# Layer 0 of a four-layer network: column-bias queries stored column by column, and the preparation of a unit in pieces of one copy

## The chip, the cores and the metric

The kernel runs on one core of a Trainium2 chip. The core has five engines with a queue each: TensorE (PE in the profile; PEld are its weight loads), VectorE (DVE), ScalarE (ACT), GpSimd (POOL) and SyncE (SP, which here only issues transfers). Each engine works through its own queue in order; semaphores order the engines among each other. Matrix products land in PSUM, which has eight banks; everything else lies in SBUF. The metric is the time of one execution in microseconds on the device, the median of several runs. Everything is computed in float32.

## The reference, cut to what matters

Four layers work on `x` of shape (2, 64, 64, 128). The change touches layer 0 alone: group norm, then attention over the 4096 positions of each image with 4 heads of 32 values, with a relative position bias of rows and one of columns:

```python
x = x + _L0_conv_ref(_gn(x), L0_conv_w_qkv, L0_conv_pos_emb_h, L0_conv_pos_emb_w)

def _L0_conv_ref(x, w_qkv, pos_emb_h, pos_emb_w):
    scale = 1.0 / float(kd) ** 0.5
    qkv = jnp.einsum('bhwc,cd->bhwd', x, w_qkv)
    q, k, v = jnp.split(qkv, [qk_dims, 2 * qk_dims], axis=-1)
    ...
    pos = relative_position_bias(pos_q, pos_emb_h, pos_emb_w).reshape(B, nh, L, L)
    scores = jnp.einsum('bnqd,bnkd->bnqk', q, k) * scale + pos
    attn = jax.nn.softmax(scores, axis=-1)
    out = jnp.einsum('bnqk,bnkd->bnqd', attn, v)
```

The bias of a query at row x, column y, for a key at row x', column y', is the query times the row embedding of x'-x plus the query times the column embedding of y'-y. So the row bias of a query is one number for each of 64 key rows, and the column bias one for each of 64 key columns.

## The kernel before

**Units and steps.** Layer 0 is `layer0` (a prologue), then `l0_bounded` (the loop). The loop has 8 units: image `b`, pair of heads, half of the queries (2048, that is 32 rows of 64). A unit has 4 blocks of 512 queries, a block 32 steps of 128 keys: 1024 steps. A step is: scores on TensorE (L615: 64-by-64 tiles, both heads, into two PSUM banks), their exponential on ACT (L623), a product with the exponentiated column bias on DVE (L626), and, two steps later, the product with the values on TensorE (L573). After 32 steps ACT copies the sums out (L582), and three small pieces finish the block (`l0_finish`).

The row bias needs no pass of its own: rows 32 to 63 and 96 to 127 of the query operand `qa` hold it, and the same rows of the key operand `ka` hold a one at the key's row (`l0_hot`, on POOL). The column bias comes in as a factor: its exponential `ew`, for 64 key columns, is multiplied in by L626.

**The preparation of a unit**, `l0_prepare`, is a generator: it stops at every `yield`, and each `piece()` of the loop runs it to the next one. It makes the operands of the next unit while the present one runs:

- queries: L657 projects two blocks of 512 positions into one bank (`l0pq`); L677 to L687 copy it into `qa`: to rows 0-31 and 64-95 as the operand proper, for both halves of the keys, and to rows 32-63 (query columns 0 to 31) and 96-127 (columns 32 to 63) as the operand of the column bias, in the same order of positions;
- column bias: for each of the 64 query columns L701 multiplies a slice of the embedding with the queries of that column (`rhs=qa[lo : lo + HD, :, y::S]`, one value in 64). Columns 0-31 come from rows 32-63 and go to one bank, columns 32-63 come from rows 96-127 and go to another; both use partitions 0-63 of their bank. L712 exponentiates each bank into `ew`, with the positions interleaved. Once all are done, a transfer on SP's queue (L715) doubles `ew` to the other 64 partitions;
- row bias: L723 multiplies for each of 32 rows, from rows 0-31 into partitions 0-63 and from rows 64-95 into partitions 64-127 of one bank (`l0ph`); L734 copies it into rows 32-63 and 96-127 of `qa`, over the copies that the column bias was made from;
- for the first half of a pair also the keys: L657 (`l0pk`) and L747, L748.

The loop calls `piece()` after every odd step; after steps 2, 6, 10 and so on it calls `more()`, which runs other generators that wait in `extra` (L1's first rows, `statistics` of finished blocks). Finishing pieces go ahead of preparing ones. PSUM in the loop: 4 banks for scores, 2 for the sums, 2 shared by everything else (`misc`).

The order on a queue isn't the order written: a planner with its own model of the engines orders each block of the program, and moves an instruction ahead where it finds the engine free. It also orders two engines that read one PSUM bank, one after the other.

**The prologue.** `Net.__init__` loads `x` with 8 transfers of 512 KB on SP's queue (L52). `layer0` loads the weights and the two embeddings on ACT's queue (L264, L282), turns the embeddings (L286) and copies them to four groups of partitions (L289), and works out an upper bound of all scores (L300 to L354; a Gram matrix of the weights and the lengths of the embeddings). For each image it then transposes `x` in 8 banks (`group_block`: L113, statistics on DVE L116, a copy on ACT L118), aggregates the statistics (`group_stats`) and normalises two halves (L395). `lengths` squares a half (L373 on POOL or L375 on ACT) and finds its longest row. In between, `pieces(4)` runs the generator of the first unit. The bound decides at run time whether `l0_bounded` or `l0_any` runs; here it is the former. Last come the values of image 0, `l0_values` (L484, L491). PSUM in the prologue: 5 banks, all under `misc`.

Of the kernel before, what the change touches and what calls it, by code (L numbers as in the profile page):

```python
# [14 lines left out]
P = 128  # L15
B = 2
# [23 lines left out]
class Net:  # L40


    def __init__(self, ctx, tc, ins, out):
# [6 lines left out]
        src = ins["x"].rearrange("b h w c -> (b h w) c").rearrange("(g p) c -> p g c", p=P)  # L50
        for g in range(0, B * NC, 8):
            nc.sync.dma_start(out=self.x[:, g : g + 8, :], in_=src[:, g : g + 8, :])  # L52
# [16 lines left out]


# [186 lines left out]
    def layer0(self, xT, gst, na, nb):  # L257
# [3 lines left out]
        with ExitStack() as st:  # L261
            wp = st.enter_context(tc.tile_pool(reuse_waits="tile", name="l0w", bufs=1))
            w = wp.tile([P, 3 * C], F32, tag="wqkv", name="wqkv")
            nc.scalar.dma_start(out=w, in_=ins["L0_conv_w_qkv"])  # L264

# [9 lines left out]
            with (  # L275
                tc.tile_pool(reuse_waits="tile", name="l0s", bufs=2) as ap,
                tc.tile_pool(reuse_waits="tile", name="l0sp", bufs=5, space=PSUM) as ps,
            ):
                raw = ap.tile([P, 2, HD], F32, tag="raw", name="l0raw")
                nc.vector.memset(raw, 0.0)  # L280
                for i, n in enumerate("hw"):
                    nc.scalar.dma_start(  # L282
                        out=raw[: 2 * S - 1, i, :], in_=ins[f"L0_conv_pos_emb_{n}"]
                    )
                    pt = ps.tile([P, 512], F32, tag="misc", name=f"l0pe{n}")
                    nc.tensor.transpose(pt[:HD, :P], raw[:, i, :], self.ident)  # L286
# [3 lines left out]
                posq = ap.tile([P, 2, HD], F32, tag="posq", name="l0posq")  # L290
                nc.vector.tensor_tensor(posq, raw, raw, ALU.mult)
                posn = ap.tile([P, 2], F32, tag="posn", name="l0posn")
                nc.vector.tensor_reduce(posn, posq, AX.X, ALU.add)
# [40 lines left out]
                for j in range(2):  # L334
# [25 lines left out]
                made = {}  # L360
                first = self.l0_prepare(
                    ps, (0, 0, 0), xT, w, pe, [ka], (qe[:, 0], qe[:, 1]), made
                )

                def pieces(n):
                    for _ in range(n):
                        next(first, None)

                def lengths(b, half):
                    part = xT[:, b, half * 2048 : (half + 1) * 2048]  # L370
                    sq = ap.tile([P, 2048], F32, tag="sq", name=f"l0sq{b}_{half}")
                    if half:
                        nc.gpsimd.tensor_tensor(sq, part, part, ALU.mult)  # L373
                    else:
                        nc.scalar.activation(sq, part, AF.Square)  # L375
# [13 lines left out]
                for b in range(B):  # L389
                    for g in range(NC // 4):  # L390
                        self.group_block(ps, gst[:, b], b, g, xT[:, b, :])
                    gm, gr = self.group_stats(ps, gst[:, b], b)
                    for half in range(2):
                        part = xT[:, b, half * 2048 : (half + 1) * 2048]
# [16 lines left out]
                for _ in first:  # L411
                    pass
# [1891 lines left out]
```

## Time and profile before

| | us |
|---|---|
| median of 3 runs | 4787.77 (4781.72 to 4788.86) |
| the profiled execution | 4783.74 |
| its span, first to last instruction | 4781.9 |
| mean granted TensorE clock | 0.963 of full speed |
| first scores of the loop (L615) | 87.41 |
| last copy of the sums (L582) | 2088.7 |

The loop of layer 0 thus takes 42% of the time, the prologue 1.8%. The units begin at 87.4, 332.2, 582.7, 829.7, 1082.1, 1355.5, 1610.7 and 1857.7 us by their first scores; the last ends at 2088.5. It is the only one that prepares nothing for a following unit.

How the page is read: busy time is the time in which an engine works, with its share of the span. The row of digits gives an engine's busy share in 40 equal slices of 119.5 us, in tenths. A line of a group names the line in the code, engine, operation, output and inputs with their shape (partitions by elements), the count, then the busy time of all of them in us and the mean of one in ns, and after the last bar the idle time of the engine just ahead of them, and which work ended it. TensorE makes two passes over a float32 product, so a product counts twice. Matmuls are pipelined: their ends are modelled, and the distance from start to start is the surer measure. In a timeline a line has start, duration, engine, line, operation, tiles, count, and in brackets the idle time before it.

### The profile page before, as it was taken

The page shows a single profiled execution, that of the slowest core. Times are in us where ns is not written, and L with a number is a line of the kernel's source. Part 1 is how long each engine was busy: PE and PEld are TensorE (multiplying, and loading weights), DVE is VectorE, ACT ScalarE, POOL GpSimd, SP SyncE. Part 2 cuts the span into 40 slices and gives each one's busy share as a digit, 9 for nine tenths or more (in the row PEclk, how much of TensorE's full clock was granted, in tenths as well). Part 3 has the DMA queues.
Part 4 walks back from the last instruction along what each step waited for, and adds up shares of the span by engine and source line. Part 5 has one row for each costly group of instructions (what it writes and reads, how often), then busy time and mean ns, then how long its engine had stood idle before and what let it go on. Part 6 is the DMA issues. An engine that isn't in the chain of part 4 may idle for free.

```text
span 4781.9 us, 76270 instructions
## 1 busy us (share of the span) xinstructions
PE 4464.8 (93%) x32236; PEld 1739.6 (36%) x32236; DVE 2943.9 (62%) x4850; ACT 2697.7 (56%) x3157; POOL 945.6 (20%) x848
## 2 busy tenths in 40 slices
PE   6999999999999999977899999999967999999999
PEld 3333333333333333335323223222224444444444
DVE  5676767677766767766755657555554444444447
ACT  5666565656666665545666766676731443433326
POOL 1000000000000000004455555555521000000008
PEclk8999999999999999988999999999978999999999
DMA  1000000000000000000000000000034000000001
GB/s 47 10 1 10 1 10 1 10 1 1 10 1 10 1 13 1 1 5 21 6 1 1 1 1 1 1 1 1 1 109 181 1 0 0 0 1 0 0 1 36
DMA packets 42562, 60.16 MB, mean 13 GB/s; under 512 B 4224, under 2 KB 24928, under 8 KB 41568
## 3 DMA queue, kind: packets, MB, share of 16 engines
q1 hardware_dynamic: 40912, 54.34, 3.7%
q8 instruction: 257, 4.21, 0.4%
q10 hardware_dynamic: 1296, 0.82, 0.1%
q14 instruction: 97, 0.79, 0.1%
HBM read 42.56 MB, written 4.19 MB: 10 GB/s over the span
## 4 chain that ended last, share of the span: by engine, by line
PE 75%; DVE 11%; ACT 7%; issue 3%; POOL 2%; DMA 1%; SPq 0%; DVEq 0%; ACTq 0%; POOLq 0%
PE l0o L573 15%; PE l0sc L615 15%; PE scl L2126 9%; PE oTl L2085 9%; PE l2sc L1498 5%; PE l2pos L1245 5%; PE l2av L1544 3%; PE f3ex L2235 2%; DVE l2es L1518 2%; POOL l2es L1521 2%; ACT l0es L623 2%; ACT l2es L1529 1%; DVE l0es L626 1%; PE l0pw L701 1%; PE l1p L988 1%
## 5 line engine op out<-in xcount | busy, mean ns | idle before, releaser
L626 DVE TENSOR_TENSOR l0es<-l0es,l0qe 128x1024 f32<-128x1024 f32 x1024 | 1250.2, 1228 | 529.5 <-ACT l0es L623 528.4
L623 ACT ACTIVATE l0es<-l0sc 128x1024 f32<-128x1024 f32 x1024 | 1044.0, 1025 | 604.5 <-PE l0sc L615 599.5
L573 PE MATMUL l0o<-l0es,l0v 64*33 64x512 f32 x8192 | 1072.9, 592 | 32.2 <-DVE l0es L626 16.7
L615 PE MATMUL l0sc<-l0qe,ka 64*64 64x512 f32 x8192 | 1080.3, 595 | 5.7 <-ACT l0es L623 5.0
L1529 ACT ACTIVATE l2es<-l2es 128x1024 f32<-128x1024 f32 (+3 forms) x576 | 559.4, 984 | 264.8 <-POOL l2es L1521 257.7
L1521 POOL TENSOR_TENSOR l2es<-l2es 128x1024 f32<-128x1024 f32 (+3 forms) x352 | 581.2, 1662 | 493.6 <-DVE l2es L1518 424.9
L2093 DVE TENSOR_TENSOR accl<-accl,esl 128x1024 f32<-128x1024 f32 x240 | 302.5, 1261 | 424.6 <-ACT esl L2137 421.2
L1518 DVE TENSOR_SCALAR l2es<-l2sc 128x1024 f32<-128x1024 f32 (+3 forms) x320 | 338.8, 1059 | 312.1 <-PE l2sc L1498 311.5
L2137 ACT ACTIVATE esl<-scl 128x1024 f32<-128x1024 f32 x240 | 245.8, 1024 | 485.0 <-PE scl L2126 451.7
L615 PEld LDWEIGHTS l0sc<-l0qe,ka 64*64 64x64 f32 x8192 | 298.5, 133 | 568.0 <-issue 490.4
L573 PEld LDWEIGHTS l0o<-l0es,l0v 64*33 64x33 f32 x8192 | 255.5, 108 | 646.6 <-issue 518.7
L2126 PE MATMUL scl<-l3qT,l3kT 128*128 128x512 f32 x1024 | 487.3, 595 | 0.0
L1498 PE MATMUL l2sc<-l2q,kept 32*128 32x512 f32 (+3 forms) x2304 | 392.2, 624 | 86.2 <-ACT l2es L1509 62.2
L2085 PE MATMUL oTl<-esl,l3v 128*128 128x512 f32 x960 | 451.1, 592 | 0.0
L776 POOL TENSOR_TENSOR x<-x,l0y 128x256 f32<-128x256 f32 x32 | 23.4, 730 | 1994.5 <-DVE l0y L771 1899.8
L1544 PE MATMUL l2av<-l2es,kept 128*32 128x512 f32 (+3 forms) x2304 | 309.5, 588 | 0.0
L1245 PE MATMUL l2pos<-kept 128*32 128x512 f32 x2416 | 295.2, 597 | 0.1
L2085 PEld LDWEIGHTS oTl<-esl,l3v 128*128 128x128 f32 x960 | 181.7, 190 | 225.6 <-issue 221.8
L2126 PEld LDWEIGHTS scl<-l3qT,l3kT 128*128 128x128 f32 x1024 | 188.2, 191 | 207.5 <-issue 191.3
L1509 ACT ACTIVATE l2es<-l2sc 128x1024 f32<-128x1024 f32 x224 | 226.3, 1010 | 52.5 <-PE l2sc L1498 51.3
L1498 PEld LDWEIGHTS l2sc<-l2q,kept 32*128 32x128 f32 x2304 | 116.9, 188 | 329.4 <-ACT l2es L1509 163.5
L1245 PEld LDWEIGHTS l2pos<-kept 128*32 128x32 f32 x2416 | 78.1, 111 | 173.8 <-issue 173.0
(707 smaller groups left out, 3748.9 us busy)
## 6 DMA issues: line engine op xcount, KB each, us to landing
f2w<-in_L_ffn_weight_dram SPq DMA_DIRECT2D x32, 1024.0 KB, 13.1
l0qe<-l0qe SPq DMA_DIRECT2D x8, 1024.0 KB, 6.7
x<-in_x_dram SPq DMA_DIRECT2D x8, 512.0 KB, 8.8
out_dram<-x SPq DMA_DIRECT2D x16, 256.0 KB, 2.3
kept<-in_L_attn_pos_rev_dram SPq DMA_DIRECT2D x1, 1792.0 KB, 6.8
ew<-in_L_ffn_expert_w_dram SPq DMA_DIRECT2D x1, 512.0 KB, 4.1
kept<-in_L_attn_pos_rev_dram SPq DMA_DIRECT2D x1, 256.0 KB
f2b<-in_L_ffn_weight_dram ACTq DMA_DIRECT2D x2, 128.0 KB, 2.6
```

The costliest lines, as they stand in the source:

```text
L573: nc.tensor.matmul(o[64 * h : 64 * h + HD + 1, r, :], lhsT=v1[rows, k, 2 * pair + h, :], rhs=es[rows, h, :], start=(k == 0), stop=(k == NC ...
L615: nc.tensor.matmul(sc[64 * c : 64 * c + 64, h, :], lhsT=ka[rows, k0 : k0 + 64], rhs=qa[rows, k // (NC // 2), qs], start=True, stop=True,)
L623: nc.scalar.activation(es, sc, AF.Exp)
L626: nc.vector.tensor_tensor(es, es, ew[:, :, qs], ALU.mult)
L1245: nc.tensor.matmul(out[part], lhsT=lhsT[:, part], rhs=rhs, start=start, stop=stop)
L1498: nc.tensor.matmul(sc[:, h2, off:], lhsT=kT[hs, k * P : (k + 1) * P], rhs=q[hs, off:], start=True, stop=True,)
L1518: nc.vector.tensor_scalar(es[:, :, lo:], sc[:, :, lo:], root, None, ALU.mult)
L1521: nc.gpsimd.tensor_tensor(part, part, part, ALU.mult)
L1529: nc.scalar.activation(es[:, :, off:], es[:, :, off:], AF.Silu)
L1544: nc.tensor.matmul(avs[i][hs, off:], lhsT=v[:, k, hs], rhs=es[h // 2][:, h % 2, off:], start=(k == 0), stop=last,)
L2085: nc.tensor.matmul(oT, lhsT=vs[b][:, k, :], rhs=es[:, i, :], start=(k == 0), stop=(k == NC - 1),)
L2126: nc.tensor.matmul(sc[:, i, :], lhsT=kTs[b][:, k * P : (k + 1) * P], rhs=qT[:, qb * 512 : (qb + 1) * 512], start=True, stop=True,)
```

## The change

1. **Queries for the column bias** are stored in `qa` column by column: the copies write them with a stride of 32 values, one column's 32 rows lie side by side, and the product reads 32 values in a row for each head. Both groups of columns now write one bank, columns 0-31 partitions 0-63 and columns 32-63 partitions 64-127, instead of two banks.
2. **The preparation yields before every copy.** `moved` runs a list of copies, in turn on ACT and DVE. A bank of queries takes 16 copies (8 of 32x512, 8 of 32x256) instead of 12 of mixed size, which were handed out two and four at a time; row biases and keys keep their copies. The two exponentials of a bank come in two calls. The loop calls `piece()` after every step, except that in steps 2, 6, 10 and so on `more()` goes first where `extra` isn't empty.
3. **The first unit** is prepared with `alone=True`: no `yield` between copies, and each bank is evicted by one engine, banks alternating between ACT and DVE. It and the first values have four PSUM banks of their own (`first`), and `misc` has four instead of five.
4. **The values** (`l0_values`) are evicted by ACT and DVE in turn.
5. **The prologue's order:** the embeddings load ahead of the weights, without a clearing of their tile; two of the eight transfers of `x` (blocks 4 and 5) go to ACT's queue; image 0 is transposed and normalised first, then image 1 transposed, then come embeddings and bound, then the norm of image 1, the lengths, and the first unit. Of the four squares POOL keeps one; ACT has three.

```diff
-        for g in range(0, B * NC, 8):
-            nc.sync.dma_start(out=self.x[:, g : g + 8, :], in_=src[:, g : g + 8, :])
+        self.load_x(nc.sync, [0, 1, 2, 3, 6, 7])
...
+            raw = wp.tile([2 * S - 1, 2, HD], F32, tag="raw", name="l0raw")
+            for i, n in enumerate("hw"):
+                nc.scalar.dma_start(out=raw[:, i, :], in_=ins[f"L0_conv_pos_emb_{n}"])
             nc.scalar.dma_start(out=w, in_=ins["L0_conv_w_qkv"])
+            self.load_x(nc.scalar, [4, 5])
...
-                tc.tile_pool(reuse_waits="tile", name="l0sp", bufs=5, space=PSUM) as ps,
+                tc.tile_pool(reuse_waits="tile", name="l0sp", bufs=4, space=PSUM) as ps,
...
+                blocks(0)
+                normed(0)
+                blocks(1)
...
-                    if half:
+                    if half and b == 0:
                         nc.gpsimd.tensor_tensor(sq, part, part, ALU.mult)
...
+                normed(1)
                 for b in range(B):
                     for half in range(2):
-                        pieces(4)
                         lengths(b, half)
...
-                for _ in first:
+                for _ in self.l0_prepare(
+                    ps, (0, 0, 0), xT, w, pe, [ka], (qe[:, 0], qe[:, 1]), {}, tag="first", alone=True
+                ):
                     pass
-                self.l0_values(ps, 0, xT, w, v)
+                self.l0_values(ps, 0, xT, w, v, tag="first")
...
-            nc.scalar.copy(
+            (nc.vector.tensor_copy if g % 2 else nc.scalar.copy)(
                 v[:, 4 * g : 4 * g + 4, :, :HD],
...
-                        if k % 2:
+                        if extra and k % 4 == 2:
+                            more()
+                        else:
                             piece()
-                        elif k % 4 == 2:
-                            more()
...
+        def moved(n, moves, scale=1.0):
+
+            for i, (dst, src) in enumerate(moves):
+                if not alone:
+                    yield
+                if (n if alone else i) % 2:
+                    nc.vector.tensor_scalar(dst, src, scale, None, ALU.mult)
+                else:
+                    nc.scalar.activation(dst, src, AF.Copy, scale=scale)
+            yield
+
         for g in range(0, H2 // 512, 2):
             pq = projected(0, half * (H2 // 512) + g, f"l0pq{t}_{g}")
+            moves = []
             for i in range(2):
                 cols = slice((g + i) * 512, (g + i + 1) * 512)
...
-                yield
-                nc.scalar.copy(qa[:64, 1, cols], pq[64 * i : 64 * i + 64])
-                nc.vector.tensor_copy(qa[:HD, 0, cols], p0)
-                yield
-                nc.vector.tensor_copy(left[0], left[1])
-                for h, p in ((0, p0), (1, p1)):
...
-                    (nc.scalar.copy if h else nc.vector.tensor_copy)(right[0], right[1])
-                nc.scalar.copy(
-                    qa[64 : 64 + HD, :, cols], p1.unsqueeze(1).broadcast_to([HD, 2, 512])
-                )
-            yield
+                for h in range(2):
+                    p = pq[64 * i + 32 * h : 64 * i + 32 * h + 32]
+                    for kh in range(2):
+                        moves.append((qa[64 * h : 64 * h + HD, kh, cols], p))
+                    for j in range(2):
+                        rows = slice(32 + 64 * j, 64 + 64 * j)
+                        dst = qa[rows, h, : H2 // 2].rearrange("p (y x) -> p x y", y=S // 2)
+                        src = p.rearrange("p (x y) -> p x y", y=S)
+                        x = slice(8 * (g + i), 8 * (g + i) + 8)
+                        moves.append((dst[:, x, :], src[:, :, 32 * j : 32 * j + 32]))
+            yield from moved(g // 2, moves)
         for g in range(4):
-            pw = [
-                ps.tile([P, 8, 2, S // 2], F32, tag="misc", name=f"l0pw{t}_{g}_{i}")
-                for i in range(2)
-            ]
+            pw = ps.tile([P, 8, 2, S // 2], F32, tag=tag, name=f"l0pw{t}_{g}")
...
-                        pw[i][:S, n, :, :],
+                        pw[64 * i : 64 * i + S, n, :, :],
                         lhsT=pe[lo : lo + HD, 1, S - 1 - y : 2 * S - 1 - y],
-                        rhs=qa[lo : lo + HD, :, y::S],
+                        rhs=qa[lo : lo + HD, :, (8 * g + n) * 32 : (8 * g + n + 1) * 32],
...
             for i in range(2):
+                if i:
+                    yield
                 y = 32 * i + 8 * g
                 dst = ew[:S].rearrange("p h (x y) -> p y h x", y=S)
-                nc.scalar.activation(dst[:, y : y + 8], pw[i][:S], AF.Exp)
+                nc.scalar.activation(dst[:, y : y + 8], pw[64 * i : 64 * i + S], AF.Exp)
...
-            yield
-            for lo in (0, 64):
-                for kh, copy in ((0, nc.scalar.copy), (1, nc.vector.tensor_copy)):
-                    copy(
+            yield from moved(
+                g,
+                [
+                    (
                         qa[lo + 32 : lo + 64, kh, cols].rearrange("p (x y) -> p x y", y=S),
                         ph[lo + 32 * kh : lo + 32 * kh + 32],
                     )
+                    for lo in (0, 64)
+                    for kh in range(2)
+                ],
+            )
...
-                yield
-                for i in range(2):
...
-                    nc.scalar.activation(ka[:HD, cols], pk[lo : lo + HD], AF.Copy, scale=root)
-                    nc.vector.tensor_scalar(
-                        ka[64 : 64 + HD, cols], pk[lo + HD : lo + 64], root, None, ALU.mult
-                    )
+                moves = [
+                    (
+                        ka[64 * h : 64 * h + HD, (g + i) * 512 : (g + i + 1) * 512],
+                        pk[64 * i + 32 * h : 64 * i + 32 * h + 32],
+                    )
+                    for i in range(2)
+                    for h in range(2)
+                ]
+                yield from moved(g // 2, moves, root)
```

## The prediction

> **What bounds the kernel now.** I read the page first: the busy shares, the slices and the chain. The first 2,090 us are layer 0.
>
> ```profile
> PE 4464.8 (93%) x32236; PEld 1739.6 (36%) x32236; DVE 2943.9 (62%) x4850; ACT 2697.7 (56%) x3157; POOL 945.6 (20%) x848
> ...
> PE   6999999999999999977899999999967999999999
> ```
>
> TensorE is 90% busy or more in every slice of layer 0 but the first (6). So in the loop a change is worth what it takes from TensorE's work or from its waits; only ahead of the loop (to 87.4 us) are other engines a candidate. Next I asked for the groups by form, from 88 to 2,092 us, because a mean by line mixes prologue and loop.
>
> ```profile
> L626 DVE TENSOR_TENSOR l0es<-l0es,l0qe 128x1024 f32<-128x1024 f32 x1024 | 1250.2, 1228 | 529.5 <-ACT l0es L623 528.4
> L623 ACT ACTIVATE l0es<-l0sc 128x1024 f32<-128x1024 f32 x1024 | 1044.0, 1025 | 604.5 <-PE l0sc L615 599.5 <-DVE l0ri L769 3.0
> L701 PE MATMUL l0pw<-l0qe,l0pe 32*64 32x64 f32 x896 | 57.3, 284 | 0.0
> L712 ACT ACTIVATE l0qe<-l0pw 64x512 f32<-64x512 f32 x56 | 54.9, 1076 | 49.3 <-PE l0pw L701 49.3
> L734 ACT COPY l0qe<-l0ph 32x512 f32<-32x512 f32 x56 | 32.3, 576 | 46.1 <-DVE l0qe L734 24.4 <-PE l0ph L723 21.7
> L723 PE MATMUL l0ph<-l0qe,l0pe 32*64 32x64 f32 x896 | 32.1, 220 | 0.0
> ```
>
> The two bias products have the same form and count, yet L701 takes 57.3 us and L723 32.1. The timeline of TensorE shows a step of the loop (L615 scores, L573 values), then both kinds of burst:
>
> ```profile
> 634.93 1.04 PE L615 MATMUL l0sc<-l0qe,ka 64*64 64x512 f32 x8
> ...
> 636.64 1.04 PE L615 MATMUL l0sc<-l0qe,ka 64*64 64x512 f32 x8
> ...
> 638.47 1.98 PE L701 MATMUL l0pw<-l0qe,l0pe 32*64 32x64 f32 x32
> 640.38 1.09 PE L615 MATMUL l0sc<-l0qe,ka 64*64 64x512 f32 x8
> ...
> 685.76 1.15 PE L723 MATMUL l0ph<-l0qe,l0pe 32*64 32x64 f32 x32
> 686.84 1.09 PE L615 MATMUL l0sc<-l0qe,ka 64*64 64x512 f32 x8
> ```
>
> An undisturbed step is 1.71 us from scores to scores. In it ACT has 1.71-1.025 = 0.69 us to spare, DVE 1.71-1.228 = 0.48. A column burst (L701) holds the scores back 640.38-638.47 = 1.91 us, a row burst (L723) 686.84-685.76 = 1.08. The last view is the same timeline at an eviction of a query bank (l0pq):
>
> ```profile
> 602.29 1.04 PE L615 MATMUL l0sc<-l0qe,ka 64*64 64x512 f32 x8
> 603.15 1.04 PE L573 MATMUL l0o<-l0es,l0v 64*33 64x512 f32 x8
> 604.24 1.09 PE L615 MATMUL l0sc<-l0qe,ka 64*64 64x512 f32 x8
> 606.08 1.06 PE L573 MATMUL l0o<-l0es,l0v 64*33 64x512 f32 x8 [0.74 <-DVE l0es L626]
> 607.30 1.09 PE L615 MATMUL l0sc<-l0qe,ka 64*64 64x512 f32 x8 [0.16 <-ACT l0es L623]
> ```
>
> Scores start at 602.29, 604.24, 607.30, then 609.44: 0.24+1.35+0.43 = 2.0 us over three plain steps. ACT runs two copies (L686, L687: 0.37 and 1.01 us) in one stretch ahead of the exponentials, DVE three.
>
> **The change, part by part.** All terms are against the profiled execution: 4783.74 us, span 4781.9. The median of the three runs is 4787.77, 4.0 above; I make no correction for that.
>
> *1. Column bursts.* The moving operand (64 columns as 2 blocks of 32, stride 256 bytes) becomes 2 blocks of 32 contiguous values, and the two row groups write separate halves of one bank, not the lower half of two. That is what L723 does (row groups 0 and 64, halves of one bank, contiguous), so I take its price: 1.91-1.08 = 0.83 us, 4 bursts in each of 7 units prepared in the loop: **-23**. The bounds: 0 if the pace comes from something else, and above now if two row groups can't share a bank (third rival). The weights stay a 32x64 slice.
>
> The Trainium skill, "TensorEngine Tiling (Array Packing)", Gotcha 1: PSUM Pressure, speaks against it: different row tiles can't access one PSUM bank at the same time. Row: L723 does so at 1.08 us a burst, writing different partitions. By the rule this term would be no gain or a loss, by the row -23; I go by the row.
>
> *2. Query evictions in the loop.* Now a bank (two halves) is 6 copies on ACT (two each of 64x512 0.58, 32x256 0.36, 32x1024 1.00: 3.9 us) and 6 on DVE (0.68+2x0.42, twice: 3.0), handed out two and four at a time. After, 16 copies, alternating ACT and DVE, one per call. Eight are 32x512: 0.576 (ACT) or 0.685 (DVE, L748's row). Eight are 32x256 written with stride 128 bytes: no such row. Lower end the contiguous 0.36 and 0.42; upper end by L712, which also writes scattered words, 1076 against 576 ns for 512: factor 1.87, so 0.68 and 0.79. Per bank ACT 3.8 to 5.0, DVE 4.4 to 5.9 us: more work, in smaller bites. One bite of ACT (0.58) fits its 0.69 spare; one of DVE (0.69) overshoots its 0.48 by 0.2, and the step after has none. The queue is not in the order written (the copies of 599 to 606 us run within four steps, though written over ten): drawn into 8 steps, DVE has 8x0.48 = 3.8 for 4.4 to 5.9, so the multiplication L626 is what becomes late next. The nearest rows are L734 and L747/L748, which already alternate the engines in copies of 0.58 and 0.69: their steps lose 0.05 us, the last of a chain 0.3 to 0.6. I take 0.5 a bank. Today's stalls, subtracted the same way for the 14 banks, sum to 29 us (5 for the first, 1.2 for two that hide behind other work, 2.0 for the rest). So 29-14x0.5 = 22: **-22**; ends -29 (no stall) and 0 (2.0 a bank again).
>
> The Trainium skill, "Advanced Engine Details and Errata", SBUF Cachelines, says an access that leaves its 16-byte line each time pays. L701 and L712 agree (1.91 and 1.076 us); for the new strided copies it would point to the upper prices, with no figure.
>
> *3. Column exponentials, row and key copies, slots.* L712 keeps count and size; two in one step lose 0.05 us now, one in a step no more. L734, L747 and L748 keep counts and sizes. A unit now needs 66 calls (86 with keys) instead of 22 (26), plus 12 for the finishing; there are 128 less at most 32: it fits, or nearly, where L1's rows share them. The copy of the exponentiated biases (SP's queue, 6.7 us to landing) is issued some 20 to 30 steps later, still 40 steps (70 us) ahead of its use. No other transfer on SP's queue stands behind it there. Zero.
>
> *4. Second batch.* Eight banks of values (7.5 us of TensorE) gain nothing from two engines: TensorE is the slower side. From 1141 to 1189 us DVE is full with layer 1's rows and the loop loses 27 us; two column bursts hide in that. If later calls push them out they cost 2x1.1, and up to 8 DVE copies (5.5 us) may fall in: **+4** (0 to +8).
>
> *5. Prologue.* The loop starts at 87.41. From 18.4 to 87.4 us ACT is busy 47.0, TensorE 49.6 at a granted clock of 0.75, DVE 39.9: no engine is full, waits order it. The first transposes (18.43) stand in TensorE's queue behind the embeddings, landed at 13.2, and the Gram chain. After, they come first: 4.2 MB of x at the 233 GB/s of that stretch take 18 us, so batch 0 is in by about 10 and its norm some 12 us earlier than 34. The first unit's query copies took 40.7 to 54.8 us for 7.8 us of ACT work, as ACT and DVE waited for each other; by one engine per bank it is the longer of 7.5 to 10.0 (ACT) and 8.8 to 11.8 (DVE). Against that: a Square (1.91) moves from POOL to ACT, four value banks (4x0.59) from ACT to DVE (4x0.69). ACT's queue also issues five DMAs, two of x, ahead of its first copy; SP's eight took 14.4 us, so about 9; batch 0's later blocks share the bandwidth with them. Up to 22 less (12 earlier, 10 less waiting), up to 3 more (if the end is ACT's work). I take the earlier start alone: **-12**.
>
> Sum: -23-22+4-12 = -53: 4783.7-53 = **4731**.
>
> **The rivals.** *DVE becomes the bound during preparation:* strided copies at the upper price, drawn together, each bank losing 2.0 as now: 4753; a microsecond more a bank, 4767. For it: DVE's 3.8 us of room. Against: L734's and L748's chains. *The layout doesn't quicken the bursts* (two blocks of 32 are not L723's 64 in a row): 4754. *Two row groups in one bank take turns:* a burst is 16 pairs in 1.91 us, 0.12 a pair; one at a time doubles it, +1.91x28 = 53 instead of -23: 4807, **slower**. It decides once a burst costs more than 1.9+30/28 = 3.0 us, since the other terms are worth 30. Against it: L723's row.
>
> **How the numbers follow.** Likeliest 0.71 (its own range: ends -74 and, with 8 left of term 2 and +3 in the prologue, -20: 4710 to 4764); DVE bound 0.12; bursts as now 0.08; turns in one bank 0.07; a queue order that loses elsewhere 0.02. The first three are faster, less 0.05 for mixtures that end within 0.2% (9.6 us, about what a measurement here can tell): 0.86, 0.05, 0.09 slower. The range takes in the first two rivals and a better prologue: 4700 to 4775.
>
> **What would show it.** Right: L701's group near 32 us instead of 57 in the loop; no step of 3 us after a query bank; the loop's first scores near 75 us. Wrong: L701 at 57 or above (layout, or turns); waits of L573 for L626 growing (DVE bound); first scores at 87 or later; a longer DVE-full stretch past 1,100 us.

## The result, and the profile after

The changed kernel takes 4816.64 us (median; 4814.06 to 4817.46), against 4787.02 for the kernel before on the same chip: a ratio of 1.0063, 95% interval 1.0045 to 1.0080. It is slower; 4731 was predicted, and 4775 was the top of the range. The profiled spans are 4814.6 and 4781.9 us, so there are 32.7 us to find. In the new kernel the lines have moved by four: scores L619 (before L615), values product L577 (L573), exponential L627 (L623), multiplication L630 (L626), copies of the preparation L676 on DVE and L678 on ACT, column products L704 (L701), row products L728 (L723).

From the page, busy time by engine, and TensorE in 40 slices:

```profile
PE 4463.7 (93%) x32236; PEld 1715.9 (36%) x32236; DVE 2983.8 (62%) x4890; ACT 2718.4 (56%) x3182; POOL 944.8 (20%) x847
...
PE   7999999998999999978799999999967999999999
```

No engine has become a bound: DVE gained 40 us over the whole span, TensorE runs the same 32236 products. The time is in waits. The groups by form, from 85 to 2120 us (busy time, mean ns of one | idle time before them and what ended it), with the scores of the kernel before, from 88 to 2092 us, ahead of them:

```profile
L615 PE MATMUL l0sc<-l0qe,ka 64*64 64x512 f32 x8192 | 1080.3, 595 | 5.7 <-ACT l0es L623 5.0
...
L619 PE MATMUL l0sc<-l0qe,ka 64*64 64x512 f32 x8192 | 1078.7, 595 | 39.5 <-ACT l0es L627 39.5
L717 ACT ACTIVATE l0qe<-l0pw 64x512 f32<-64x512 f32 x56 | 59.2, 1057 | 27.8 <-PE l0pw L704 27.1
L676 DVE TENSOR_SCALAR l0qe<-l0pq 32x512 f32<-32x512 f32 x56 | 38.4, 686 | 4.0 <-ACT l0qe L678 2.6
L678 ACT ACTIVATE l0qe<-l0pq 32x256 f32<-32x256 f32 x56 | 33.8, 603 | 59.3 <-DVE l0qe L676 59.3
L676 DVE TENSOR_SCALAR l0qe<-l0pq 32x256 f32<-32x256 f32 x56 | 33.4, 597 | 27.7 <-ACT l0qe L678 27.2
L704 PE MATMUL l0pw<-l0qe,l0pe 32*64 32x64 f32 x896 | 32.1, 220 | 0.0
L728 PE MATMUL l0ph<-l0qe,l0pe 32*64 32x64 f32 x896 | 32.1, 220 | 0.0
```

Two things are to be seen. The column products L704 now cost what the row products cost, 32.1 us: the first term came true. And TensorE's scores wait 39.5 us for the exponential on ACT (5.7 before), while ACT stood idle 59.3 us in sum ahead of its strided copies, waiting for copies of DVE's. The timeline at a query bank shows the two together (start, duration, engine, line; in brackets the idle time before and what ended it):

```profile
636.26 0.69 DVE L676 TENSOR_SCALAR l0qe<-l0pq 32x512 f32<-32x512 f32 x1
636.28 1.06 PE L577 MATMUL l0o<-l0es,l0v 64*33 64x512 f32 x8
636.98 0.59 ACT L678 ACTIVATE l0qe<-l0pq 32x256 f32<-32x256 f32 x1 [1.40 <-DVE l0qe L676]
637.60 1.02 ACT L627 ACTIVATE l0es<-l0sc 128x1024 f32<-128x1024 f32 x1
...
638.64 0.59 ACT L678 ACTIVATE l0qe<-l0pq 32x512 f32<-32x512 f32 x1
638.65 1.23 DVE L630 TENSOR_TENSOR l0es<-l0es,l0qe 128x1024 f32<-128x1024 f32 x1 [0.47 <-ACT l0es L627]
638.67 1.09 PE L619 MATMUL l0sc<-l0qe,ka 64*64 64x512 f32 x8 [1.32 <-ACT l0es L627]
639.91 0.69 DVE L676 TENSOR_SCALAR l0qe<-l0pq 32x512 f32<-32x512 f32 x1
...
640.63 0.59 ACT L678 ACTIVATE l0qe<-l0pq 32x256 f32<-32x256 f32 x1 [1.39 <-DVE l0qe L676]
641.24 1.02 ACT L627 ACTIVATE l0es<-l0sc 128x1024 f32<-128x1024 f32 x1
```

Follow ACT from 637.60. The exponential ends at 638.62; the multiplication on DVE needs it and ends at 639.88; behind the multiplication stands DVE's copy, to 640.60; ACT's next copy of the same bank waits for that copy, to 641.22; and behind ACT's copy stands the next exponential, at 641.24. That is a ring through two queues: 1.02 + 1.23 + 0.69 + 0.59 and some gaps of 0.03 make 3.64 us for a step that takes 1.72 undisturbed. From 639.23 to 640.63 ACT does nothing, although the scores for its next exponential are ready at 639.76.

Accounts, as what a step takes above 1.717 us, with the price of what else TensorE does in it taken off: a bank of queries costs 4.8 to 6.0 us (2.0 before). In the six units other than 4 and the last the banks cost 39 us more, the column bursts 20 less, and the steps behind column bursts 8 more, +27 in sum. Unit 4, where the second batch's values and layer 1's rows fall in, is 7 longer, the first scores come 2.6 earlier (84.8 us), and what follows the loop is 1.3 longer. That is 32.6 of them.

### The profile page after: what moved, and what is told of

It reads as the page before. It is cut to its first block, busy times and chain, and to the rows that moved or that the text cites. A ratio compares the mean times of both kernels' runs of the same rounds, so it can differ in the third digit from the quotient of the medians.

```text
span 4814.6 us, 76316 instructions
## 1 busy us (share of the span) xinstructions
PE 4463.7 (93%) x32236; PEld 1715.9 (36%) x32236; DVE 2983.8 (62%) x4890; ACT 2718.4 (56%) x3182; POOL 944.8 (20%) x847
## 4 chain that ended last, share of the span: by engine, by line
PE 73%; DVE 11%; ACT 8%; issue 4%; POOL 3%; DMA 0%; POOLq 0%; ACTq 0%; DVEq 0%
PE l0o L577 15%; PE l0sc L619 15%; PE scl L2136 9%; PE oTl L2095 9%; PE l2sc L1508 5%; PE l2pos L1255 5%; PE l2av L1554 3%; DVE l0es L630 2%; ACT l0es L627 2%; PE f3ex L2245 2%; DVE l2es L1528 2%; POOL l2es L1531 2%; ACT l2es L1539 1%; PE l1p L998 1%; ACT l0qe L678 1%
## 5 line engine op out<-in xcount | busy, mean ns | idle before, releaser
L630 DVE TENSOR_TENSOR l0es<-l0es,l0qe 128x1024 f32<-128x1024 f32 x1024 | 1250.4, 1229 | 496.9 <-ACT l0es L627 495.4
L627 ACT ACTIVATE l0es<-l0sc 128x1024 f32<-128x1024 f32 x1024 | 1040.8, 1024 | 587.6 <-PE l0sc L619 581.5
L619 PE MATMUL l0sc<-l0qe,ka 64*64 64x512 f32 x8192 | 1078.7, 595 | 39.5 <-ACT l0es L627 39.5
L577 PE MATMUL l0o<-l0es,l0v 64*33 64x512 f32 x8192 | 1072.9, 592 | 40.7 <-ACT l0os L586 21.6
L619 PEld LDWEIGHTS l0sc<-l0qe,ka 64*64 64x64 f32 x8192 | 296.8, 133 | 599.6 <-issue 461.0
L577 PEld LDWEIGHTS l0o<-l0es,l0v 64*33 64x33 f32 x8192 | 248.2, 108 | 672.6 <-issue 471.1
```

The lines of the kernel that those rows point to most:

```text
L577: nc.tensor.matmul(o[64 * h : 64 * h + HD + 1, r, :], lhsT=v1[rows, k, 2 * pair + h, :], rhs=es[rows, h, :], start=(k == 0), stop=(k == NC ...
L619: nc.tensor.matmul(sc[64 * c : 64 * c + 64, h, :], lhsT=ka[rows, k0 : k0 + 64], rhs=qa[rows, k // (NC // 2), qs], start=True, stop=True,)
L627: nc.scalar.activation(es, sc, AF.Exp)
L630: nc.vector.tensor_tensor(es, es, ew[:, :, qs], ALU.mult)
```

## The experiments

Times of three rounds have an interval; the others are one execution, read for their timeline. "Loop" runs from the first scores to the last values product: 2001.1 us before, 2035.1 after.

**One copy a step.** The first theory, A, was that the planner draws the sixteen copies of a bank together, though they are handed out one a step, and that a dense stretch is what costs. In the kernel after, each copy of a query bank in the loop keeps its place in the program's order:

```diff
+                if pin and not alone:
+                    self.tc.keep_in_program_order(ins)
...
-            yield from moved(g // 2, moves)
+            yield from moved(g // 2, moves, pin=True)
```

> The changed kernel, with each copy of a query bank in the loop ordered behind the exponential or multiplication of its own step (issue order only, no new wait), so that the 16 copies of a bank lie over some 16 steps instead of 5. Theory A (the 16 copies are drawn together into five steps, two a step on ACT and two on DVE, and that is the stall): the 5.9 us that a bank loses now (1.6+1.9+1.9+0.4) fall to 1 or less; 14 banks make some 65 us, so about 4750 us (4740 to 4770), faster than both. Rival B (the copies cost what they cost wherever they stand, as there are more of them and the strided ones are slow): 4805 to 4820, the loss spread over more steps.

Measured: 4758.72 us, ratio 0.9936 (0.9919 to 0.9953), loop 1971.2: 64 us less than after, 30 less than before. Outside unit 4 most steps with a copy lose 0.00 to 0.05 us; some 0.2 goes where a bank's last copies meet the projection of the next, and up to 0.8 where they meet a column burst. The group of scores, in the loop:

```profile
L619 PE MATMUL l0sc<-l0qe,ka 64*64 64x512 f32 x8180 | 1075.7, 593 | 0.4 <-ACT l0es L627 0.4
```

The copies themselves are what they were (ACT 0.584 and 0.622 us, DVE 0.685 and 0.597). So their number and their stride don't cost the time; their place in the queues does. Whether it is density or something in the order, this run can't say.

**Storage by rows again.** After, with the queries stored in order of positions and the strided product, still in one bank:

```diff
-                        dst = qa[rows, h, : H2 // 2].rearrange("p (y x) -> p x y", y=S // 2)
+                        at = slice(32 * j, 32 * j + 32)
+                        dst = qa[rows, h, cols].rearrange("p (x y) -> p x y", y=S)
...
-                        rhs=qa[lo : lo + HD, :, (8 * g + n) * 32 : (8 * g + n + 1) * 32],
+                        rhs=qa[lo : lo + HD, :, y::S],
```

> The changed kernel without the column storage: queries for the column bias in order of positions (copies of 256 contiguous rows of 32: ACT 0.36, DVE 0.42 us instead of 0.60), the product reads one value in 64; one bank, separate halves, pieces and prologue as changed. Theory A (number of copies drawn together): a bank still loses 4 to 5 us. Rival C (the price of the strided writes): a bank loses 2.5 or less. The column burst: 1.9 us if the stride of the read sets its pace, 1.1 if the halves of the bank do. Time by A with the stride: 4817+23-14 = about 4826; by C: about 4791.

Measured: 4826.54 us, ratio 1.0083 (1.0066 to 1.0100), loop 2046.2. Bursts lose 2.02 us again, banks 3.8 and 5.1. The contiguous copies are shorter (ACT 0.376, DVE 0.423), but the stall falls by only 1.0 a bank: the strided write was the smaller part of it.

**The storage alone.** Before, with only the new storage and the single bank for the columns; copies handed out three and four at a time, prologue as before:

```diff
-                nc.scalar.copy(qa[:64, 1, cols], pq[64 * i : 64 * i + 64])
+                nc.scalar.copy(qa[:HD, 1, cols], p0)
+                nc.scalar.copy(*column(slice(32, 64), 1, p1, 0))
...
-                nc.vector.tensor_copy(left[0], left[1])
+                nc.vector.tensor_copy(*column(slice(32, 64), 0, p0, 0))
```

> The kernel before with the column storage and the one bank alone: copies handed out as before (7 a half instead of 6, as the 64x512 copy has to be split: ACT 2.8 us a half, DVE 1.9), prologue as before. Term 1 of the prediction: -23 us from the bursts (1.91 to 1.08). Theory A: 14 copies instead of 16, so a bank loses nearly what it does in the changed kernel, 4 to 5 us against 2.0: 4787-23+35 = about 4799. If only the alternation of engines copy by copy loses the time, a bank loses 2 to 2.5: about 4768.

Measured: 4807.81 us, ratio 1.0044 (1.0030 to 1.0058), loop 2018.6; bursts 1.19, banks 3.7 to 5.3 (64.6 in sum against 28.9). So the storage alone already loses more at the banks than it wins at the bursts. Twelve copies a bank became fourteen, eight of them written with a stride; which of the two costs more there wasn't taken apart. First scores came at 92.4 us.

**Column products in two banks.** After, with the two row groups writing the lower halves of two banks, contiguous reads:

```diff
-            pw = ps.tile([P, 8, 2, S // 2], F32, tag=tag, name=f"l0pw{t}_{g}")
+            pw = [
+                ps.tile([P, 8, 2, S // 2], F32, tag=tag, name=f"l0pw{t}_{g}_{i}")
+                for i in range(2)
+            ]
```

> The changed kernel with the column products of the two row groups again in two banks, both in partitions 0 to 63, read in a row. If the stride of the read set the old pace, a burst holds the scores back 1.1 us as in the changed kernel, time about 4817. If both groups writing the same partitions set it, 1.9 us, time about 4840.

Measured: 4804.02 us, loop 2028.6, bursts 1.19 us, banks as in after. With this run the four combinations are there: strided reads lose 2.01 us (two banks, before) and 2.02 (one bank, storage by rows), contiguous reads 1.19 in two banks and in one. One burst of TensorE in the storage-by-rows run (one bank, strided):

```profile
677.22 1.98 PE L704 MATMUL l0pw<-l0qe,l0pe 32*64 32x64 f32 x32
```

and one with two banks, contiguous:

```profile
683.53 1.15 PE L707 MATMUL l0pw<-l0qe,l0pe 32*64 32x64 f32 x32
```

The stride of the read sets the pace, and where the products land doesn't matter. What two banks win (6.5 us) is the step behind the burst: two exponentials out of one bank took 2.14 us in a row on ACT, out of two banks 1.93 to 1.96, and the third step behind a one-bank burst came 0.3 us late; with two banks that is gone. Why one bank makes the pair longer wasn't tried.

**The same pinning in the kernel before.** It separates density from order, since before hands out two and four copies at a time:

```diff
+        def kept(ins):
+            if unit != (0, 0, 0):
+                self.tc.keep_in_program_order(ins)
...
-                nc.scalar.copy(qa[:64, 1, cols], pq[64 * i : 64 * i + 64])
+                kept(nc.scalar.copy(qa[:64, 1, cols], pq[64 * i : 64 * i + 64]))
```

> The kernel before with one thing changed: in all units but the first, each copy out of a query bank keeps its place in the program's order, behind its step's exponential and multiplication. Copies, layout and bursts are as before. Theory A (a bank's stall is made by several copies standing together in ACT's and DVE's queues): the stall of a bank falls from 2.0 us to 0.5 or less, the loop from 2001 us by 22 to 28 to about 1976, column bursts stay at 2.0 us a step, and the time comes out near 4762. If the copies were already spread and the 2.0 us are what the copies cost wherever they stand: the loop stays near 2001 us and the time near 4787.

Measured: 4804.16 us, ratio 1.0038 (1.0024 to 1.0053), loop 2019.4; the two banks of a unit lose 5.7 to 5.8 us together, 7.5 in the second unit (before: 3.4 to 4.1, and 6.5 in the first unit), and more in unit 4, where layer 1's rows fall in. Slower, where theory A had it faster and its rival the same. The timeline of its second piece:

```profile
630.05 1.22 DVE L626 TENSOR_TENSOR l0es<-l0es,l0qe 128x1024 f32<-128x1024 f32 x1 [0.36 <-ACT l0es L623]
...
631.31 0.41 DVE L684 COPY l0qe<-l0pq 32x256 f32<-32x256 f32 x1
...
631.75 0.42 DVE L690 COPY l0qe<-l0pq 32x256 f32<-32x256 f32 x1
...
632.20 0.36 ACT L690 COPY l0qe<-l0pq 32x256 f32<-32x256 f32 x1 [2.18 <-DVE l0qe L690]
632.59 1.00 ACT L692 COPY l0qe<-l0pq 32x1024 f32<-32x1024 f32 x1
633.62 1.94 ACT L623 ACTIVATE l0es<-l0sc 128x1024 f32<-128x1024 f32 x2
```

ACT is idle for 2.18 us: its copy waits for DVE's two copies of the same bank, which stand behind the multiplication. Spread over eight to ten steps instead of four, the banks cost more in every unit but the first, so density over a bank isn't it. That brought theory H: a stall is a hand-off of one bank from engine to engine within a step, with the next exponential queued behind it. Three runs test it.

**One copy a step in the kernel before.** As the last, with a `yield` after every copy.

```diff
                 kept(nc.scalar.copy(qa[:64, 1, cols], pq[64 * i : 64 * i + 64]))
+                yield
                 kept(nc.vector.tensor_copy(qa[:HD, 0, cols], p0))
```

> The kernel before with its query-bank copies kept in program order as in e5_before_pinned, but every copy is a piece of its own. In e5_before_pinned a piece held two copies on DVE and then two on ACT: ACT's copy waited 2.18 us for DVE's, which stood behind the step's multiplication, and the next exponential stood behind ACT's copy. Theory H (a stall is such a hand-off of one bank from engine to engine within one step): with one copy a step the other engine's copy is long done, only the 1.00-us copy on ACT oversteps its 0.69 us of room, by 0.3, twice a bank. Stall 0.5 to 1.0 a bank instead of 2.0, loop 1980 to 1988 us, time 4766 to 4776. If keeping the copies in program order is itself what cost in e5_before_pinned: loop 2019 us or more, time 4804 or more.

Measured: 4756.78 us, ratio 0.9937 (0.9921 to 0.9954), loop 1972.7. Banks lose 0.0 to 0.3 us, but for two in unit 4 whose copies meet layer 1's rows (some 10, and 0.9); first scores came at 83.7. So pinning as such doesn't cost. The 1.00-us copy, expected to lose 0.3, loses nothing; that the scores have two buffers, so that a single late exponential is absorbed, would explain it but wasn't tried. The kernel before, with nothing but its copies spread, is as fast as the changed kernel with its copies spread (4756.78 and 4758.72).

**Two copies a step, ACT first.** After, pinned, in pairs:

```diff
-                if not alone:
+                if not (alone or (pin and i % 2)):
                     yield
```

> The pinned kernel of the first experiment, with the copies of a query bank handed out two a step, the one on ACT first and then the one on DVE. Theory H: ACT's copy waits for DVE's copy of the step before, which is nearly done; the loop of exponential, multiplication, copy on DVE, copy on ACT (1.02+1.23+0.69+0.59 and some waits, 3.65 us) closes once in two steps, 1.83 us a step against 1.72, so about 0.1 a step, 1 us a bank, and the loop is 1971 us plus 10 to 15. Density theory (what counts is how many copies lie on a step): ACT's copy fits its room, DVE's 0.64 oversteps 0.48 by 0.16, 1.3 us a bank at most: the same here.

**Two copies a step, DVE first.** The same pairs, the order in a pair turned round:

```diff
-                if (n if alone else i) % 2:
+                if (n if alone else i + pin) % 2:
```

> As e10_pairs_act_first, with the two copies of a step in the other order: the one on DVE first, then the one on ACT. The same number of copies on each engine in each step. Density theory: as e10_pairs_act_first, within some microseconds. Theory H: ACT's copy waits for DVE's copy of the same step, which stands behind the multiplication, which waits for the exponential; the next exponential stands behind ACT's copy. The loop of 3.65 us closes once a step: 1.9 us lost in each of 8 steps, 15 us a bank, 215 us in 14 banks; loop near 2185 us, time near 4980.

Measured: 4754.45 us and loop 1975.7 with ACT first, 4935.84 us and loop 2153.5 with DVE first. The two kernels put the same number and sizes of copies on the same engines and steps, and their loops differ by 178 us. A step with ACT first:

```profile
584.76 0.69 DVE L676 TENSOR_SCALAR l0qe<-l0pq 32x512 f32<-32x512 f32 x1
...
585.48 1.23 DVE L630 TENSOR_TENSOR l0es<-l0es,l0qe 128x1024 f32<-128x1024 f32 x1
585.48 0.62 ACT L678 ACTIVATE l0qe<-l0pq 32x256 f32<-32x256 f32 x1 [0.34 <-DVE l0qe L676]
586.13 1.02 ACT L627 ACTIVATE l0es<-l0sc 128x1024 f32<-128x1024 f32 x1
```

and one with DVE first:

```profile
640.79 0.69 DVE L676 TENSOR_SCALAR l0qe<-l0pq 32x512 f32<-32x512 f32 x1
...
641.51 0.59 ACT L678 ACTIVATE l0qe<-l0pq 32x512 f32<-32x512 f32 x1 [2.01 <-DVE l0qe L676]
642.12 1.02 ACT L627 ACTIVATE l0es<-l0sc 128x1024 f32<-128x1024 f32 x1
...
643.17 1.22 DVE L630 TENSOR_TENSOR l0es<-l0es,l0qe 128x1024 f32<-128x1024 f32 x1 [1.70 <-ACT l0es L627]
```

With ACT first, its copy waits 0.34 us for DVE's copy of the step before, and steps lose 0.00 to 0.09, where 0.1 was expected; only where a bank's last copies meet the next projection (0.2) or a column burst (0.6 to 1.8, outside unit 4) is more lost. With DVE first it waits 2.01 for the copy of its own step, and once a bank is under way each step with a pair loses some 1.84 (strided copies) or 1.93 us: the ring of 3.65, once a step, as in the kernel after. The forecast of 4980 was 44 too high: outside unit 4 the units are 25 to 28 us longer than with one copy a step, 13 to 14 a bank where 15 was expected, as a bank's first steps lose only 0.5 to 0.9. Density theory (A), which had the two alike, falls. The group of scores goes with it: from 80 to 2240 us they wait 0.4 us for the exponential with ACT first and 98.4 with DVE first.

**The first unit's banks by both engines.** After, with the copies of the first unit alternating:

```diff
-                if (n if alone else i) % 2:
+                if i % 2:
```

> The kernel after with one thing changed: the first unit's copies go to ACT and DVE by turns instead of a bank to one engine. If the second bank, whose copies all stand in DVE's queue behind the norms and lengths (30.3 to 52.5 us), is what keeps the first scores back at 84.8 us: first scores at 81 us or earlier. If two engines that read one bank hold each other up, or if the end of the preparation is set by the chain of lengths and bounds: 84.8 us or later. Loop 2035 us either way.

Measured: 4819.41 us, first scores at 85.9 (84.8), loop 2033.7. One engine a bank is worth 1 us there at most; the second bank, long as it took, doesn't keep the scores back.

The two prologues also show what orders the copies. Both banks are copied into the same `qa`, so the wait could come from the shared bank or from the shared destination. In the kernel after, with a bank to each engine, ACT's last ten copies run without a gap while DVE writes the same `qa`:

```profile
34.48 5.78 ACT L678 ACTIVATE l0qe<-l0pq 32x256 f32<-32x256 f32 x10
34.81 0.58 DVE L676 TENSOR_SCALAR l0qe<-l0pq 32x256 f32<-32x256 f32 x1
```

With the copies of a bank by turns, ACT waits again:

```profile
38.18 0.68 DVE L676 TENSOR_SCALAR l0qe<-l0pq 32x512 f32<-32x512 f32 x1
...
38.90 0.59 ACT L678 ACTIVATE l0qe<-l0pq 32x256 f32<-32x256 f32 x1 [0.64 <-DVE l0qe L676]
```

It is the shared bank.

**Two banks for the columns, and the values alone.** The pinned kernel with two banks, and no preparation in the first six steps of unit 4:

```diff
+                        if b and (pair, half, qb) == (0, 0, 0) and k < 6:
+                            pass
-                        if extra and k % 4 == 2:
+                        elif extra and k % 4 == 2:
```

> The pinned kernel of the first experiment, with the column products in two banks (both lower halves, contiguous read) as in the fourth, and with no piece of preparation in the first six steps of unit 4, so that the values of the second batch have both work banks to themselves. By the measured parts: 6.5 us less of the 0.3-us steps after column bursts, and in unit 4 the values cost 7 to 8 us instead of 15.4: loop 1971 us less 14, near 1957, and a time near 4744. If the values' 15.4 us are the price of their matmuls and copies rather than of a missing bank: loop near 1965 and 4752.

Measured: 4743.74 us, ratio 0.9912 (0.9896 to 0.9929), loop 1960.0. Unit 4 is 5.6 us shorter (272.1 against 277.7), unit 5 0.1, the other prepared ones 0.8 to 1.2: the values' steps lose 8.2 us instead of 15.0. A query bank that is held for twenty steps, as spreading its copies does, leaves everything else one work bank; here the values had to make do with it.

**Layer 1's rows in program order.** The last kernel, with the row work beside unit 4 kept where it was written:

```diff
-        nc.vector.tensor_tensor(y, self.x[:, n0 : n0 + 4, :], row[0], ALU.subtract)
+        kept(nc.vector.tensor_tensor(y, self.x[:, n0 : n0 + 4, :], row[0], ALU.subtract))
```

> The kernel of the run e7_more with the row work of layer 1 (norms, row statistics, normalisation), which runs in unit 4 beside the loop, kept in program order too, so that a piece lies on every fourth step instead of all of it within steps 27 to 42. If dense drawing is also what makes unit 4 the longest (some 27 us over its steps there, about 30 us of DVE work drawn together): unit 4 falls by 15 to 20 us, to about 250, units 4 and 5 grow by 3 together at most otherwise, and the time is 15 to 18 us under e7_more. If the row work costs the same wherever it lies, because DVE has no room for it: unit 4 loses what unit 5 gains, and the time is that of e7_more.

Measured: 4726.32 us, ratio 0.9873 (0.9857 to 0.9890), the fastest of all. Unit 4 fell by 11.7 us to 260.4, unit 5 grew by 0.9: the loop is 10.9 shorter, less than the 15 expected. The rest of the 17 us came from the stretch behind the loop (2693.0 against 2700.6), which the edit doesn't touch.

**The first unit ahead of the second batch.** The last kernel, with the call that prepares the first unit moved up, from behind the bound to right behind the embeddings' copies:

```diff
+                for _ in self.l0_prepare(
+                    ps, (0, 0, 0), xT, w, pe, [ka], (qe[:, 0], qe[:, 1]), {}, tag="first", alone=True
+                ):
+                    pass
                 posq = ap.tile([2 * S - 1, 2, HD], F32, tag="posq", name="l0posq")
```

> The kernel of e8_rows_pinned, with the first unit's preparation written ahead of the second batch's norm and lengths (right behind the embeddings), its copies kept in program order. In the kernel after, the second batch's norm came at 47.3 us (40.2 before), because its square root stood on ACT behind the first unit's 16 copies, and TensorE's first column burst (54.41 us) stood behind the products of that batch's lengths (to 54.48 us); from that burst to the first scores TensorE was busy nearly throughout, 30.4 us. If this order is what kept the prologue at 85 us instead of the predicted 75: the first burst comes near 42 us, the lengths' 4 us of products go behind it, first scores at 76 to 79 us (82.8 in e8_rows_pinned), loop as there (1949 us), time near 4721. If the chain of the second batch's norm, lengths and bound is what the end waits for, wherever it stands: first scores at 83 us or later.

The kernel after, where the prologue stood (ACT's copies of the first unit end at 40.26; x is normed for the second batch at 47.34):

```profile
40.28 0.20 ACT L370 ACTIVATE l0root<-l0root 1x4 f32<-1x4 f32 x1
...
40.52 0.15 DVE L372 TENSOR_TENSOR l0root<-l0root 1x1 f32<-1x1 f32 x1 [1.22 <-ACT l0root L370]
40.59 0.20 DVE L137 SCALAR_TENSOR_TENSOR gv<-gd,gmv 128x1 f32<-128x1 f32 x1
...
41.73 0.20 ACT L102 ACTIVATE rs_s<-rs_v 128x1 f32<-128x1 f32 x1 [1.01 <-DVE rs_v L98]
...
47.34 2.60 DVE L295 TENSOR_SCALAR xT<-xT,gm,gr 128x2048 f32<-128x2048 f32 x2
48.78 3.71 ACT L384 ACTIVATE l0sq<-xT 128x2048 f32<-128x2048 f32 x2 [6.85 <-DVE xT L295]
...
50.74 3.73 PE L387 MATMUL l0n<-l0sq,l0ones 128*32 128x512 f32 x16 [5.67 <-ACT l0sq L384]
...
54.41 1.86 PE L704 MATMUL l0pw<-l0qe,l0pe 32*64 32x64 f32 x29
```

and with the first unit ahead:

```profile
41.43 4.26 PE L714 MATMUL l0pw<-l0qe,l0pe 32*64 32x64 f32 x64 [10.39 <-DVE l0qe L681]
...
74.50 2.60 DVE L295 TENSOR_SCALAR xT<-xT,gm,gr 128x2048 f32<-128x2048 f32 x2
...
85.48 1.98 PE L622 MATMUL l0sc<-l0qe,ka 64*64 64x512 f32 x8 [2.17 <-DVE bok_l L252]
```

Measured: 4733.52 us, ratio 0.9888 (0.9872 to 0.9905), first scores at 85.5 against 82.8 without the move, loop 1951.7. The first burst came at 41.43, as expected, and TensorE was through with the unit and the first values at 71.2; but now the second batch's norm came at 74.5, and its lengths and bound ended only at 85. Two chains end the prologue: the unit's, 30 us of TensorE's work from the first burst on, and the batch's, from its statistics' first product (69.39) to the scores 16 us (85.48). In the kernel after the unit stands behind the batch, here the batch behind the unit; neither order lets them run beside each other. Copies out of the first unit's banks would have to lie between the steps of the batch's chain; that wasn't tried.

## Why the prediction was wrong

**Term 1, column bursts, -23: right.** The loss of a burst went from 2.01 to 1.19 us, 28 times. The reason given, stride or halves, is now told apart: it is the stride. The rule weighed against it, from the Trainium skill, "TensorEngine Tiling (Array Packing)", Gotcha 1: PSUM Pressure, that different row tiles can't access a bank at once, doesn't show here. Bursts lose 1.19 us in one bank as in two, where the two row groups write different partitions.

**Term 2, evictions of queries, -22: wrong, and the step that failed.** Measured: +39 in the six units other than 4 and the last. The step is "I take 0.5 a bank", taken from L734's and L747's chains, and ahead of it the bound from DVE's room, 8x0.48 us. The sizes of the copies were right: a bank is 4.8 us of ACT and 5.1 of DVE, within the ranges given. But room on each engine was the wrong question. The text knew that two engines reading one bank are ordered one after the other, and used it for the prologue alone. In the loop that order closes a ring through the queues, exponential, multiplication, DVE's copy, ACT's copy, and costs 1.9 us in each step where it closes; the 2.0 a bank of the kernel before was already such hand-offs, as they go when its copies are handed out one a step. The four copies of L734 lose 0.05 us a step where they lie, between bursts; sixteen in a row, drawn into five steps, lose up to 1.95 a step. Its ends, -29 and 0, left out a loss: 0 was "2.0 a bank again", and nothing excluded more; a microsecond more a bank stood in a rival alone.

**Term 3, 0: too low by 8.** The calls fit the steps, as said. The pair of exponentials out of one bank is what was missed: 0.05 us was taken, some 0.3 measured in the third step behind a burst.

**Term 4, second batch, +4 (0 to +8): open.** Unit 4 is 6.9 longer as a whole, though its four column bursts, at 0.82 each, take 3.3 off; what is left, some 10 us, is terms 2 to 4 together, where they had some +2 for this unit. They can't be told apart, for, as feared, values met a query bank: the step of the values lost 14.2 us, 7.6 before.

**Term 5, prologue, -12 (-22 to +3): sign right, mis-sized,** -2.6. The first batch was normed at 27.8 us, 6 earlier and not 12: DVE's first statistics started at 11.95, behind an operation that waits for the embeddings (10.79). And the second batch was normed at 47.3, 7 later than before (40.2). Its small steps stand in DVE's queue among the first unit's copies, the maxima of the first batch's lengths and the bound's L372, which waits 1.22 us for a root on ACT (40.28) behind that engine's sixteen copies. Those sixteen alone aren't the cause: with the copies by turns the norm came at 47.49. It wasn't taken apart further.

**The rivals.** Turns in one bank (4807, slower) came nearest the time, for a reason that didn't hold. "DVE becomes the bound" had the place right, copies drawn together, but the mechanism wrong (DVE has idle time in the step) and the price: "a microsecond more a bank" was three to four. "A queue order that loses elsewhere" had 0.02; it is what happened, not elsewhere but in the very steps the change rearranged. Of the signs named ahead, the column products' group near 32 us came; steps of 3 us behind a query bank didn't go, they became 3.65; first scores near 75 didn't come. The sign for a full DVE, waits of L577 for L630, tells nothing: its weight loads waited 148.9 us (82.4 before), but 158.0 in the pinned kernel, where the stalls are gone, and its products 16.6 (16.7 before). What goes with the stalls is the wait of the scores for the exponential: 5.7 before, 39.5 after, 0.4 pinned.

The nearest the runs come to the storage's own price: with copies spread, two banks and the values alone, the loop is 1960.0; the kernel before with copies spread has 1972.7. In the six prepared units other than unit 4 that is 14.4 less, in unit 4 1.8 more. The two kernels differ in the number of copies and in the values too, so this isn't the storage alone.

## What to carry to other kernels

When two in-order engines share readers of one buffer and are ordered one after the other, price the ring, not each engine's spare time: list what stands ahead of each copy on its queue, and see whether the wait closes on itself within one step. Copies of the same sizes in the same steps cost next to nothing with one engine first and up to 1.9 us a step with the other first. What is handed out a step at a time isn't issued so unless it is pinned; compare queue order before believing a price taken from a sparser stretch.

## What the runs showed of the hardware

A matmul's moving operand read at a stride of 256 bytes ran 32 products in 1.98 us; 32 values side by side took 1.15, whatever banks and partitions they went to. A copy of 256 values on 32 partitions, written at a stride of 128 bytes, took 0.603 us on ACT and 0.597 on DVE (kernel after), against 0.376 and 0.423 contiguous (storage-by-rows run); the Trainium skill, "Advanced Engine Details and Errata", SBUF Cachelines, says that accesses leaving their 16-byte line pay each time, which both pairs agree with. And the stretch behind the loop, the same in every kernel, took 2690 to 2707 us; in the pinned kernel, at 2707, the granted clock was 0.91 in a window of 700 us behind the loop where after had 0.93. Differences of some 10 us between two kernels are better read from the stretch that was edited than from the total.
